# Charges of an attention block: repeated over partitions through memory in place of copies and transposes, with new ranks for the order of work

## The chip, the cores and the metric

The kernel runs on one core of a Trainium2 chip, in one launch. Its time is the device time in microseconds; shown are medians of several runs. Its engines are TensorE (PE; the loading of its weights is shown apart as PEld), VectorE (DVE), ScalarE (ACT), GpSimd (POOL) and SyncE (SP), which here does nothing but issue DMAs. Each engine runs its own list of instructions in a fixed order and waits where an operand is not ready.

## The reference

Two blocks with residuals, in float32, over x of 32 x 512 x 256:

```python
# attention; b, n, d = 32, 512, 256
q     = tanh(x @ W_charge.T + b_charge)[..., 0]        # one charge per token
phi_c = mags * q[..., None] ** arange(5)               # its powers 0..4
shell = normalize(x @ W_shell.T + b_shell)             # 64 per token
proj  = shell @ omega.T + rff_bias                     # 32 per token
phi_s = concat([cos(proj), sin(proj)]) * rff_scale     # 64 per token
tp    = (phi_c[..., :, None] * phi_s[..., None, :]).reshape(b, n, 320)
phi   = tp @ W_combine.T                               # 64 per token
logits = einsum('bnd,bmd->bnm', phi, phi) * T / temp   # T: decay by distance
attn  = softmax(where(causal, logits, -inf))
out   = (attn @ (x @ W_v.T + b_v)) @ W_out.T + b_out
# slots
h     = gelu(concat([x, mean of S]) @ w1.T + b1)
alpha = softmax over the top 8 of 64 of (h @ w2.T + b2), else 0
slot_input = einsum('bts,btd->bsd', alpha, x) / sums   # 64 slots per batch
S_new = GRU(slot_input, S)
out   = (alpha @ (S_new @ wv.T + bv)) @ wo.T + bo
# the whole
x = x + attention(layernorm(x));  x = x + slots(layernorm(x))
```

The charge q of a token multiplies 64 values of the same token. Where the 64 values lie along the partitions, q has to be there 64 times too.

## The kernel before

The 32 batches are worked in 16 groups of two (`GB = 2`). A group has 2 x 512 tokens, `GT = 8` tiles of 128 tokens. W_out is folded into W_v in the setup, wv and wo likewise.

*Tokens and angles of a group g.* Loads bring x (and, from group 2 on, a second copy xb that VectorE transposes to xT, L876; in the first two groups TensorE does it, pta L853). TensorE projects each token tile: pf, 128 x 321 = 64 shell values, one charge before tanh, 256 values of V (L906). VectorE scales by the layernorm's statistics (bna, L786) and adds the bias: sv (L919), with tokens on the partitions. Then two strands run from sv:

- *The charges.* POOL copies the charge column 64 times, for two half-batches next to each other (qrep, L945, four copies of 128x128); TensorE transposes these in four pieces (ptq, L965), which puts 64 equal rows per half on the partitions; ACT makes Tanh (L975) and Square (L983) of the 128x512 result: qs.
- *The angles.* POOL squares the shell (sq, L992), VectorE sums (rn, L1006), POOL takes the power -1/2 (L1012, L1013), VectorE scales (shn, L1020, two halves), TensorE transposes (pts, L1036) and multiplies by omega (pp, L1053, tiles of 64x64), ACT adds the bias (ang, L1066), VectorE brings into one turn (L1077, L1078), ACT takes the Sin (L1085).

The two meet on VectorE in the powers (L1099, two instructions): tp = phases x q, x q². TensorE combines five powers (pph, L1111, 40 matmuls of 64x64 tiles), VectorE multiplies by part of the decay (phi, L1126).

*Attention.* Four row blocks per batch: logits pl (L1165), masked with their extremes by VectorE (lg, L1194), Exp on ACT (pr, L1206), transposed by TensorE (ptp, L1243) and copied by ACT (prT, L1261), times V (po, L1249), added to x by VectorE (L1278).

*Slots.* Second layernorm (lnb on POOL, xm on ACT, L1301), transposed (ptb L822, xmT L834), ph (L1328), gelu h_t (L1339), router logits prr (L1353) with their transposes rlT and prt (L1359, L1367, L1376), the top 8 by VectorE (top, L1384), their softmax on ACT and VectorE (L1393 to L1411) and al on POOL (L1418). Then psi (slot_input, L1442), gi and its transpose pt_gi (L1466), the GRU's gates prz and pn (L1492), hn (L1553) with its transpose pt_hn, al transposed (pta, L1563), pv (L1580), py (L1600), the add to x (L1614) and the store (L1619).

*The order of the work.* Nothing runs in the order in which the code is written. `Plan.add` (L126) collects steps, each with an engine, a cost, the steps it comes after and the buffers it uses. `Plan.order` (L150 to L240) gives each a rank,

```python
at = (1.0 - LATE) * s.at + LATE * (longest - s.tail)
s.rank = s.g * STRIDE + at + delay + late * max(0, s.g - last + 3)
```

where `s.at` is the earliest start within the group by the costs (with HOP for each change of engine), `s.tail` the work behind it, and delay and late come from `DELAY` for each of twelve stages. Then it simulates: of the steps whose inputs are there it places the one that could start first, among equals the one of lowest rank (TABLE is what another ACT table costs in this simulation, SWITCH what is added to a PE step's rank that has another tile shape). Buffers come from pools of fixed sizes (`SLOTS_OF`, L53). The list that results is emitted as it stands (L1645 to L1647). So a group's work overlaps with that of its neighbours, and with other costs or ranks all engines' lists come out otherwise, also far from the line that was changed.

Nearly all DMAs are on SP's list: the setup's weights (L277), x and xb, and the stores. A few weights are on ACT's and POOL's.

Of the kernel before, what the change touches and what calls it, by code (L numbers as in the profile page):

```python
# [11 lines left out]
AF = mybir.ActivationFunctionType  # L12
# [3 lines left out]
P = 128  # L16
D = 256
KD = D // P
T = 512
HT = T // 2  # L20
NT = T // P
GB = 2
GT = GB * NT
# [4 lines left out]
PHI_S = 2 * RFF  # L28
# [19 lines left out]
C_Q = SHELL  # L48
# [16 lines left out]
    "prT": 3,  # L65
    "h_t": 2,
    "qs": 1,
    "row": 7,
    "half": 4,
}  # L70


HOP = 0.41
TABLE = 1.28
SWITCH = 1.77
STRIDE = 26.98
LATE = 0.0

DELAY = {
    "setup": (0.0, 0.0),  # L80
    "load": (4.9, -6.0),
    "tokens": (10.7, 1.0),
    "angles": (-1.4, -34.3),
    "phi": (3.9, 0.9),
    "weights": (-3.0, 1.9),
    "values": (17.8, -4.4),
    "normal": (17.2, 16.3),
    "router": (34.1, 12.7),
    "taken": (-19.4, 7.1),
    "gru": (-29.8, 4.8),  # L90
    "given": (20.5, 17.4),
}

SPARE = 3
# [149 lines left out]
def block_kernel(ctx: ExitStack, tc: tile.TileContext, a: dict, out: bass.AP):  # L244
    nc = tc.nc
# [10 lines left out]
    def lazy(tag, name, shape, dtype=F32):  # L256

        if tag not in pools:
            kind = {"space": bass.MemoryType.PSUM} if tag == "ps" else {}
# [77 lines left out]
    ident = const("ident", [P, P])  # L337
# [52 lines left out]
    s_ident = add("POOL", 0.5, make_ident, rank=-41.0)  # L390
# [138 lines left out]
    for q in range(P // SQ):  # L529
        for k in range(KD):  # L530
# [9 lines left out]
                    land=4.0,  # L540
# [348 lines left out]
    def features(g):  # L889
# [45 lines left out]

        qrep = lazy("row", f"qrep_{g}", [P, GB, NT // 2, 2, PHI_S])
        sq = lazy("row", f"sq_{g}", [P, GT, SHELL])
        rn = small(f"rn_{g}", [P, GT])  # L940
        shn = lazy("row", f"shn_{g}", [P, NT, GB, SHELL])
        def repeated(bb):
            for h in range(2):
                lo = bb * NT + (h ^ bb) * (NT // 2)
                nc.gpsimd.tensor_copy(  # L945
                    qrep()[:, bb, :, h, :],
                    sv()[:, lo : lo + NT // 2, C_Q : C_Q + 1].to_broadcast([P, NT // 2, PHI_S]),
                )

        s_rep = [  # L950
            add(
                "POOL",
                0.63,
                lambda bb=bb: repeated(bb),
                s_sv[bb * NT : (bb + 1) * NT],
                [qrep, sv],
            )
            for bb in range(GB)
        ]
        ptq = bank(f"ptq_{g}")  # L960
        qs = lazy("qs", f"qs_{g}", [P, 2, T])

        def charges_turned():
            for c in range(NT):
                nc.tensor.transpose(  # L965
                    ptq()[:, c * P : (c + 1) * P],
                    qrep()[:, c // 2, c % 2].rearrange("p h s -> p (h s)"),
                    ident,
                )

        s = add("PE", 0.45, charges_turned, s_rep + [s_ident], [qrep, ptq, qs])
        s = add(
            "ACT",
            0.61,
            lambda: nc.scalar.activation(qs()[:, 0, :], ptq(), AF.Tanh),  # L975
            [s],
            [ptq, qs],
            "exp",
        )
        s_q = add(  # L980
            "ACT",
            0.62,
            lambda: nc.scalar.activation(qs()[:, 1, :], qs()[:, 0, :], AF.Square),  # L983
            [s],
            [qs],
        )

        s_sq = [
            add(
# [21 lines left out]
        def norms():  # L1011
# [80 lines left out]
        for m in (1, 3):  # L1092

            def powers(m=m):
                if m == 1:
                    a, b = tp()[:, 0:1, :].to_broadcast([P, 2, T]), qs()
                else:
                    a, b = tp()[:, 1:3, :], qs()[:, 1:2, :].to_broadcast([P, 2, T])
                nc.vector.tensor_tensor(tp()[:, m : m + 2, :], a, b, ALU.mult)  # L1099
# [6 lines left out]
        def combined():  # L1106
            for m in range(ORDER + 1):
# [32 lines left out]
    def attention(g, sv, s_sv, phi, s_phi):  # L1140
# [8 lines left out]
        for tiles in ((0, 1), (2,), (3,)):  # L1149
# [34 lines left out]
            for bb in range(GB):  # L1184
                lg = lazy("lg", f"lg_{n}_{bb}", [P, T])
                pr = lazy("pr", f"pr_{n}_{bb}", [P, T])
                prs.append(pr)
                for i in tiles:
                    nm = small(f"nm_{g}_{bb}_{i}", [P, 1], bufs=8)
                    w = (i + 1) * P  # L1190
                    c = slice(off[i], off[i] + w)

                    def lowest(bb=bb, w=w, c=c, pls=pls, lg=lg, nm=nm):
                        nc.vector.tensor_tensor_reduce(  # L1194
                            out=lg()[:, c],
                            in0=pls[bb]()[:, c],
                            in1=mask[:, T - w : T],
                            scale=1.0,
                            scalar=TOP,
                            op0=ALU.add,  # L1200
                            op1=ALU.min,
                            accum_out=nm(),
                        )
# [226 lines left out]
    def slots(g, xm, al, s_al):  # L1430
# [161 lines left out]
        for c2 in range(NT // 2):  # L1592
# [16 lines left out]
            for bb in range(GB):  # L1609
# [97 lines left out]
```

## Time and profile before

| | |
|---|---|
| time, median of 3 runs | 717.17 us (716.65 to 717.93) |
| time of the profiled execution | 716.61 us |
| its span | 714.8 us |
| granted clock of TensorE, mean | 0.993 |
| busy: PE | 686.8 us (96%) |
| busy: DVE / ACT / POOL | 595.3 / 422.5 / 236.2 us |
| ptq (L965), 64 transposes of 128x128 | 9.7 us by durations, 274 ns each (they overlap) |
| qrep (L945), 64 copies on POOL | 17.8 us, 294 ns each |
| Tanh L975 / Square L983, 16 each on ACT | 9.7 / 10.2 us |
| powers (L1099), 32 on DVE | 39.4 us, 1231 ns each |
| DMA moved | 53.76 MB |

A group's row in the profile gives: line, engine, operation, output <- inputs, shapes, count, then busy time in all, the mean of one in ns, and after the bar how long the engine stood idle just ahead of these instructions and for whom. Idle time matters only on the engine that sets the end at that place. Rows of matmuls (PE) give durations from start to end; as matmuls overlap, the pitch from one to the next is shorter. In a chain row, "PE pl L1165 x16" is a run of 16 instructions of one kind, with its start and its length.

### The profile page before, as it was taken

Reading aid. Unit: us, or ns where it says so; the run is one execution under the profiler, and the core shown is the slowest. Engines: PE = TensorE matmul, PEld = TensorE weight load, DVE = VectorE, ACT = ScalarE, POOL = GpSimd, SP = SyncE. Lnnn points to the kernel's source line nnn. Section 1 sums busy time; section 2 is a strip of 40 time slices with the busy share of each in tenths; the row PEclk is TensorE's granted clock in tenths of the full one; section 3 lists DMA queues with packets and bytes.
Section 4 is the critical chain, followed back from the end, with each engine's and each line's share of the span. In section 5 each row is a group of like instructions: output and inputs, shape, how many; then the busy total and the mean of one; then the engine's idle time right before and its main releaser. Section 6 shows DMA issues by size and latency. Waiting matters only on the chain.

```text
span 714.8 us, 12300 instructions
## 1 busy us (share of the span) xinstructions
PE 686.8 (96%) x4170; PEld 480.2 (67%) x4170; DVE 595.3 (83%) x1750; ACT 422.5 (59%) x867; POOL 236.2 (33%) x470
## 2 busy tenths in 40 slices
PE   3989999999999999999999999999999999999884
PEld 3757676767676766767676776767667676777453
DVE  3999888789798989979897979979899887878474
ACT  1445849585755747656565856467475655758720
POOL 3640532214334432324324133423423243321120
PEclk9999999999999999999999999999999999999989
DMA  6796113032304223331412333131330301001013
GB/s 179 161 278 121 34 26 60 2 118 58 119 2 115 63 60 118 60 120 25 94 59 60 119 60 118 27 93 60 59 118 1 118 1 60 1 1 60 0 60 118
DMA packets 100016, 53.76 MB, mean 75 GB/s; under 512 B 64017, under 2 KB 99153, under 8 KB 99953
## 3 DMA queue, kind: packets, MB, share of 16 engines
q1 hardware_dynamic: 98640, 52.45, 28.3%
q8 instruction: 33, 0.54, 0.3%
q10 hardware_dynamic: 1104, 0.36, 0.2%
q0 software_dynamic: 208, 0.17, 0.2%
q14 instruction: 31, 0.25, 0.1%
HBM read 35.85 MB, written 16.78 MB: 74 GB/s over the span
## 4 chain that ended last, share of the span: by engine, by line
PE 89%; DVE 4%; ACT 2%; DMA 2%; issue 1%; POOL 1%; DVEq 0%; ACTq 0%; POOLq 0%
PE po L1249 20%; PE pf L906 18%; PE ph L1328 7%; PE pl L1165 5%; PE pph L1111 5%; PE ptp L1243 5%; PE psi L1442 4%; PE py L1600 4%; PE ptb L822 4%; PE prz L1492 4%; PE pv L1580 2%; PE prr L1353 2%; PE pn L1492 2%; PE pta L1563 1%; DMA x<-in_x_dram 1%; PE pp L1053 1%
## 5 line engine op out<-in xcount | busy, mean ns | idle before, releaser
L1249 PE MATMUL po<-sv,prT 128*128 128x256 f32 x640 | 149.6, 380 | 0.0
L906 PE MATMUL pf<-wfb,xT 128*128 128x321 f32 x448 | 133.2, 439 | 0.0
L1249 PEld LDWEIGHTS po<-sv,prT 128*128 128x128 f32 x640 | 117.0, 189 | 22.6 <-issue 5.9
L906 PEld LDWEIGHTS pf<-wfb,xT 128*128 128x128 f32 x448 | 80.4, 190 | 37.5 <-issue 6.8
L1301 ACT ACTIVATE xm<-x,lnb 128x256 f32<-128x256 f32 x128 | 66.0, 594 | 43.3 <-POOL lnb L807 43.3
L1206 ACT ACTIVATE pr<-lg,nm 128x128 f32<-128x128 f32 (+3 forms) x128 | 70.7, 555 | 13.1 <-DVE nm L1194 9.8
L1278 DVE SCALAR_TENSOR_TENSOR x<-po,den,x 128x256 f32<-128x256 f32 x128 | 60.3, 475 | 20.3 <-PE po L1249 20.0
L945 POOL COPY qrep<-sv 128x128 f32<-128x128 f32 x64 | 17.8, 294 | 154.1 <-DVE sv L919 154.1
L919 DVE SCALAR_TENSOR_TENSOR sv<-pf,lna,bias_f 128x321 f32<-128x321 f32 x128 | 63.8, 543 | 4.3 <-PE pf L906 3.9
L1194 DVE CUSTOM_DVE_ANT_0 lg<-pl,mask 128x128 f32<-128x128 f32 (+3 forms) x128 | 55.9, 487 | 6.9 <-PE pl L1165 6.8
L1328 PE MATMUL ph<-xmT,w1x 128*128 128x512 f32 x128 | 59.5, 596 | 0.0
L786 DVE BATCH_NORM_STATS2 bnb<-x 128x6 f32<-128x256 f32 x128 | 53.3, 424 | 3.1
L1261 ACT COPY prT<-ptp 128x384 f32<-128x384 f32 (+1 forms) x96 | 45.9, 517 | 4.9 <-PE ptp L1243 4.7
L786 DVE BATCH_NORM_STATS2 bna<-x 128x6 f32<-128x256 f32 x128 | 46.9, 413 | 0.0
L1243 PE MATMUL ptp<-ident,pr 128*128 128x128 f32 x320 | 45.4, 274 | 0.4 <-ACT pr L1206 0.3
L1243 PEld LDWEIGHTS ptp<-ident,pr 128*128 128x128 f32 x320 | 37.1, 140 | 8.5 <-ACT pr L1206 2.4
L1614 DVE TENSOR_TENSOR x<-py,x 128x512 f32<-128x512 f32 x64 | 39.9, 684 | 3.3 <-PE py L1600 3.0
L834 ACT COPY xmT<-ptb 128x512 f32<-128x512 f32 x64 | 33.3, 589 | 15.8 <-PE ptb L822 15.8
L1165 PE MATMUL pl<-phi 64*128 64x256 f32 (+1 forms) x384 | 42.4, 356 | 0.0
L797 POOL TENSOR_TENSOR lnb<-bnb 128x8 f32<-128x8 f32 x16 | 9.8, 612 | 94.4 <-DVE bnb L786 94.4
L1099 DVE TENSOR_TENSOR tp<-tp,qs 128x1024 f32<-128x1024 f32 x32 | 39.4, 1231 | 1.3 <-ACT tp L1085 0.7
L876 DVE STREAM_TRANSPOSE xT<-xb 128x512 f32<-128x512 f32 x56 | 38.2, 695 | 0.5 <-issue 0.4
(171 smaller groups left out, 1291.7 us busy)
## 6 DMA issues: line engine op xcount, KB each, us to landing
x<-in_x_dram SPq DMA_DIRECT2D x32, 512.0 KB, 4.8
out_dram<-x SPq DMA_DIRECT2D x64, 256.0 KB, 2.5
xb<-in_x_dram SPq DMA_DIRECT2D x112, 128.0 KB, 3.4
setup<-in_gru_whh_t_dram SPq DMA_DIRECT2D x1, 768.0 KB, 4.6
wih<-in_gru_wih_t_dram SPq DMA_DIRECT2D x1, 768.0 KB, 7.9
wfb<-wf SPq DMA_DIRECT2D x8, 40.1 KB, 3.4
setup<-in_W_v_dram SPq DMA_DIRECT2D x1, 256.0 KB, 3.5
setup<-in_W_out_t_dram ACTq DMA_DIRECT2D x1, 256.0 KB, 9.2
```

The costliest lines, as they stand in the source:

```text
L786: lambda t=t: nc.vector.bn_stats(st()[:, t, :], src()[:, t, :]),
L906: nc.tensor.matmul(pf()[:, 0:NF], tile_()[:, k, c * P : (c + 1) * P], w[:, k, :], start=(k == 0), stop=(k == KD - 1),)
L919: lambda t=t, pf=pf: nc.vector.scalar_tensor_tensor(sv()[:, t, :], pf()[:, 0:NF], ln()[:, 1, t : t + 1], bias_f, ALU.mult, ALU.add,),
L1165: nc.tensor.matmul(pls[bb]()[:, off[i] + lo : off[i] + lo + w], phi()[r, 0, q : q + P], phi()[r, 1, k : k + w], start=True, stop=True,)
L1194: nc.vector.tensor_tensor_reduce(out=lg()[:, c], in0=pls[bb]()[:, c], in1=mask[:, T - w : T], scale=1.0, scalar=TOP, op0=ALU.add, op1=ALU.min,
L1206: nc.scalar.activation(pr()[:, c], lg()[:, c], AF.Exp, bias=nm(), scale=-1.0, accum_out=den()[:, tiles.index(i), bb : bb + 1],)
L1243: nc.tensor.transpose(pt()[:, j : j + P], prs[bb]()[:, j : j + P], ident)
L1249: nc.tensor.matmul(po()[:, d * D : (d + 1) * D], pr_t()[:, lo : lo + P], sv()[:, bb * NT + j, C_V:NF], start=(j == 0), stop=(j == i),)
L1261: lambda width=width, pt=pt, pr_t=pr_t: nc.scalar.copy(pr_t()[:, 0:width], pt()[:, 0:width]),
L1278: nc.vector.scalar_tensor_tensor(xt()[:, t, :], po()[:, d * D : (d + 1) * D], den()[:, d, bb : bb + 1], xt()[:, t, :], ALU.mult, ALU.add,)
L1301: lambda t=t: nc.scalar.activation(xm()[:, t, 0:D], xt()[:, t, :], AF.Identity, bias=ln()[:, 4, t : t + 1], scale=ln()[:, 1, t : t + 1],),
L1328: nc.tensor.matmul(ph(), w1x[:, k, :], tiles[k](), start=(k == 0), stop=(k == KD - 1))
```

## The change

The charges and their squares are made on the narrow form, tokens on the partitions, 8 columns per group: ACT's Tanh reads sv's charge column (128x8), a Square follows, into qc. SP stores qc to a small tile in the chip's memory, qd, in token order: 2 x 2 x 512 values of 4 bytes, where neighbours in memory come from neighbouring partitions. Four reads on SP bring it back into qs, each to 64 partitions from the same 2 x 256 values (64 x 2 KB = 128 KB). The powers wait for all four. The four POOL copies, the four transposes with their PSUM bank and the two wide activations of each group are gone. There are two qd tiles and, as before, one qs.

The planner's constants are others too: HOP, SWITCH, STRIDE, LATE and all of DELAY, and the costs of four kinds of VectorE steps. They alter the order on all engines.

```diff
@@ SLOTS_OF
     "qs": 1,
+    "qd": 2,
...
-HOP = 0.41
+HOP = 0.65
 TABLE = 1.28
-SWITCH = 1.77
-STRIDE = 26.98
-LATE = 0.0
+SWITCH = 1.57
+STRIDE = 23.49
+LATE = 0.83
...
 DELAY = {
     "setup": (0.0, 0.0),
-    "load": (4.9, -6.0),
-    "tokens": (10.7, 1.0),
-    "angles": (-1.4, -34.3),
-    "phi": (3.9, 0.9),
-    "weights": (-3.0, 1.9),
-    "values": (17.8, -4.4),
-    "normal": (17.2, 16.3),
-    "router": (34.1, 12.7),
-    "taken": (-19.4, 7.1),
-    "gru": (-29.8, 4.8),
-    "given": (20.5, 17.4),
+    "load": (5.6, -11.7),
+    "tokens": (-1.8, -13.0),
+    "angles": (-0.8, -5.4),
+    "phi": (17.1, 3.6),
+    "weights": (29.9, -16.3),
+    "values": (27.9, -17.7),
+    "normal": (-0.4, -1.6),
+    "router": (36.0, 14.4),
+    "taken": (-24.9, -2.4),
+    "gru": (25.5, -10.5),
+    "given": (27.0, -5.8),
 }
...
-        qrep = lazy("row", f"qrep_{g}", [P, GB, NT // 2, 2, PHI_S])
...
-        def repeated(bb):
-            for h in range(2):
-                lo = bb * NT + (h ^ bb) * (NT // 2)
-                nc.gpsimd.tensor_copy(
-                    qrep()[:, bb, :, h, :],
-                    sv()[:, lo : lo + NT // 2, C_Q : C_Q + 1].to_broadcast([P, NT // 2, PHI_S]),
-                )
...
-        s = add("PE", 0.45, charges_turned, s_rep + [s_ident], [qrep, ptq, qs])
+        qc = small(f"qc_{g}", [P, 2, GT])
+        qd = lazy("qd", f"qd_{g}", [2, GB, T])
+        qs = lazy("qs", f"qs_{g}", [P, 2, GB, HT])
         s = add(
             "ACT",
-            0.61,
-            lambda: nc.scalar.activation(qs()[:, 0, :], ptq(), AF.Tanh),
+            0.25,
+            lambda: nc.scalar.activation(qc()[:, 0, :], sv()[:, :, C_Q], AF.Tanh),
+            s_sv,
+            [sv, qc],
+            "exp",
+        )
+        s = add(
+            "ACT",
+            0.2,
+            lambda: nc.scalar.activation(qc()[:, 1, :], qc()[:, 0, :], AF.Square),
             [s],
-            [ptq, qs],
-            "exp",
-        )
...
+        s = add(
+            "SP",
+            0.6,
+            lambda: nc.sync.dma_start(
+                out=qd().rearrange("m b (c p) -> p (m b c)", p=P),
+                in_=qc().rearrange("p m t -> p (m t)"),
+            ),
             [s],
-            [qs],
-        )
+            [qc, qd],
+            land=3.5,
+        )
+        s_q = []
+        for h in range(2):
+            for bb in range(GB):
+
+                def repeated(h=h, bb=bb):
+                    lo = (h ^ bb) * HT
+                    nc.sync.dma_start(
+                        out=qs()[h * PHI_S : (h + 1) * PHI_S, :, bb, :],
+                        in_=qd()[:, bb, lo : lo + HT].partition_broadcast(PHI_S),
+                    )
+
+                s_q.append(add("SP", 0.6, repeated, [s], [qd, qs], land=3.0))
...
-                0.4,
+                0.35,
                 lambda bb=bb: nc.vector.tensor_tensor(
                     shn()[:, :, bb, :],
...
-            s_tp.append(add("DVE", 1.25, powers, [s_tp[-1], s_q], [tp, qs]))
+            s_tp.append(add("DVE", 1.25, powers, [s_tp[-1]] + s_q, [tp, qs]))
...
-                0.42,
+                0.35,
                 lambda h=h, n=n, dec=dec: nc.vector.tensor_tensor(
                     phi()[:, n, h * HT : (h + 1) * HT],
...
-                        "DVE", 0.17 + 0.12 * (i + 1), lowest, [s_pl, s_mask], [pls[bb], lg, nm]
+                        "DVE", 0.11 + 0.12 * (i + 1), lowest, [s_pl, s_mask], [pls[bb], lg, nm]
...
-                s_y = add("DVE", 0.65, added, [s], [pys[bb], xt])
+                s_y = add("DVE", 0.6, added, [s], [pys[bb], xt])
```

More of the change, by code (lines that the diff above doesn't have):

```diff
@@ L258, in lazy @@
         if tag not in pools:
-            kind = {"space": bass.MemoryType.PSUM} if tag == "ps" else {}
+            space = {"ps": bass.MemoryType.PSUM, "qd": bass.MemoryType.DRAM}.get(tag)
+            kind = {"space": space} if space else {}
             pools[tag] = ctx.enter_context(
@@ L941, in features @@
         shn = lazy("row", f"shn_{g}", [P, NT, GB, SHELL])
-        def repeated(bb):
-            for h in range(2):
-                lo = bb * NT + (h ^ bb) * (NT // 2)
-                nc.gpsimd.tensor_copy(
-                    qrep()[:, bb, :, h, :],
-                    sv()[:, lo : lo + NT // 2, C_Q : C_Q + 1].to_broadcast([P, NT // 2, PHI_S]),
-                )
[L950 to L956, printed above, removed]
-            )
-            for bb in range(GB)
-        ]
@@ L960, in features @@
[L960 to L968, printed above, removed]
-                )
-        s = add("PE", 0.45, charges_turned, s_rep + [s_ident], [qrep, ptq, qs])
+        qc = small(f"qc_{g}", [P, 2, GT])
+        qd = lazy("qd", f"qd_{g}", [2, GB, T])
@@ L972, in features @@
+        qs = lazy("qs", f"qs_{g}", [P, 2, GB, HT])
         s = add(
             "ACT",
-            0.61,
-            lambda: nc.scalar.activation(qs()[:, 0, :], ptq(), AF.Tanh),
-            [s],
-            [ptq, qs],
+            0.25,
+            lambda: nc.scalar.activation(qc()[:, 0, :], sv()[:, :, C_Q], AF.Tanh),
+            s_sv,
+            [sv, qc],
             "exp",
         )
-        s_q = add(
+        s = add(
             "ACT",
-            0.62,
-            lambda: nc.scalar.activation(qs()[:, 1, :], qs()[:, 0, :], AF.Square),
+            0.2,
+            lambda: nc.scalar.activation(qc()[:, 1, :], qc()[:, 0, :], AF.Square),
@@ L984, in features @@
             [s],
-            [qs],
+            [qc],
         )
+        s = add(
[5 more added lines that the diff above has]
+            ),
+            [s],
+            [qc, qd],
[11 more added lines that the diff above has]
+                s_q.append(add("SP", 0.6, repeated, [s], [qd, qs], land=3.0))
@@ L1094, in powers @@
             def powers(m=m):
+                q = qs().rearrange("p m b t -> p m (b t)")
                 if m == 1:
-                    a, b = tp()[:, 0:1, :].to_broadcast([P, 2, T]), qs()
+                    a, b = tp()[:, 0:1, :].to_broadcast([P, 2, T]), q
                 else:
-                    a, b = tp()[:, 1:3, :], qs()[:, 1:2, :].to_broadcast([P, 2, T])
+                    a, b = tp()[:, 1:3, :], q[:, 1:2, :].to_broadcast([P, 2, T])
                 nc.vector.tensor_tensor(tp()[:, m : m + 2, :], a, b, ALU.mult)
-            s_tp.append(add("DVE", 1.25, powers, [s_tp[-1], s_q], [tp, qs]))
+            s_tp.append(add("DVE", 1.25, powers, [s_tp[-1]] + s_q, [tp, qs]))
         plan.stage = "phi"
```

## The prediction

> **What bounds the kernel now.** I read the page's first part, then the busy time by stretches, then the chain of work that ended last. The page's first part, busy time by engine:
>
> ```profile
> PE 686.8 (96%) x4170; PEld 480.2 (67%) x4170; DVE 595.3 (83%) x1750; ACT 422.5 (59%) x867; POOL 236.2 (33%) x470
> ```
>
> Two stretches (length; busy time and count of PE, PEld, DVE, ACT, POOL; granted clock, DMA share, GB/s):
>
> ```profile
> 60.00:655.00 595.00, 594.96 (x3696) 420.88 (x3695) 514.89 (x1516) 376.54 (x778) 199.94 (x392) 1.00 0.25 64
> 655.00:714.80 59.80, 45.26 (x224) 26.56 (x222) 33.27 (x107) 23.26 (x43) 10.91 (x19) 0.94 0.15 53
> ```
>
> From 60 to 655 us TensorE is busy 594.96 of 595 us at full clock: there the time is the sum of its matmuls' pitches, and what other engines save is worth nothing. The rest is the fill (first matmul at 11.1 us, PE not dense before 60) and the drain (14.5 us of PE idle after 655).
>
> The chain inside the dense stretch (start, length, what):
>
> ```profile
> 275.37 2.36 PE pf L906 x8
> 277.73 1.72 PE pl L1165 x16
> ...
> 285.44 0.59 PE pta L1563 x4
> 286.02 0.33 PE ptp L1243 x3
> 286.35 0.44 PE ptq L965 x4
> 286.79 0.22 PE pt_gi L1466 x2
> ...
> 318.06 2.17 PE pf L906 x8
> ```
>
> All are PE pieces, each starting where the last ends. The transposes that go, ptq, are one piece of 0.44 us in each of 16 groups. The two pf pieces hold eight equal matmuls; the one of 2.17 us follows ptb, of the same 128x128 tile shape, the one of 2.36 us follows pl, with tiles of 64 rows. So a change of tile shape in PE's order costs 0.19 us. Over all 168 changes from 60 to 655 us the matmuls' starts in the trace stand 30.7 us over their plain pitches: **0.183 us each**.
>
> **The change, part by part.** The sum is made against the profiled span of 714.8 us. That run took 716.6, 1.8 us of it outside the span; the median shown is 717.17. So time = span + 2.4.
>
> *Removed.* From the groups by line:
>
> ```profile
> L983 ACT ACTIVATE qs<-qs 128x512 f32<-128x512 f32 x16 | 10.2, 639 | 0.3
> ...
> L965 PE MATMUL ptq<-ident,qrep 128*128 128x128 f32 x64 | 9.7, 274 | 0.0
> L975 ACT ACTIVATE qs<-ptq 128x512 f32<-128x512 f32 x16 | 9.7, 605 | 1.2 <-PE ptq L965 1.1
> ```
>
> PE: 16 x 0.44 = **-7.1 us**, on the path (the 274 ns overlap; the chain's 0.44 for four counts). POOL's 64 copies of 294 ns (17.8 us) and ACT's 32 wide activations (19.9 us) lie beside a dense PE, as does the PSUM bank that comes free: 0.
>
> *Added, narrow Tanh and Square (128x8).* No row is that narrow; nearest are the setup's 128x1 activations, 0.20 to 0.24 us: 32 x 0.21 = 6.7 us of ACT. Six more table loads (60 in the program's order for 54; 1.283 us each) add 7.7. ACT ends 5.5 us lighter at 59% busy: 0. Behind the Tanh stand two xmT copies, the router's Exp and the softmax; it waits for sv of the last token tile, done 0.5 us after the pf end, before ACT has made the xmT copies ahead of it (+3.0): it holds nobody up.
>
> *Added, the write (16 x 8 KB) and reads (64 x 128 KB) on SP.* From the page's DMA parts:
>
> ```profile
> q10 hardware_dynamic: 1104, 0.36, 0.2%
> ...
> out_dram<-x SPq DMA_DIRECT2D x64, 256.0 KB, 2.5
> xb<-in_x_dram SPq DMA_DIRECT2D x112, 128.0 KB, 3.4
> ```
>
> The reads have xb's size: 3.4 us to landing, after four issues of 0.5. The write moves 2048 single elements of 4 bytes, 128 on each of 16 engines; before writes no elements to memory. Nearest is ACT's queue, where 384 of 1104 packets have 4 bytes: 0.2% of 16 x 714.8 us over 1104 = 21 ns a packet. 128 x 21 ns = 2.7, on a store's 2.5: **5.2 us**. The Trainium skill speaks against this write: "DMA: Bandwidth & Descriptors", Rules for kernel authors, turns a strided last dimension into one descriptor per element, and by its Specifications an engine reads, modifies and writes below 512 B. If that doubles the packet's time, landing is an estimated 8 us; from below 2.5. I take 5.2, by the nearer row.
>
> Is it hidden? In the new PE order of a middle group, counted from the end of the eight pf, PE does pt_hn 0.22, pl 1.0, ptb 1.75, pl 0.8, two ph 3.44, pv 0.86, ptp 0.87, pl 0.8, pts 0.44, psi 1.89, py and pp 2.5, pt_gi and pta 0.7, ptp 0.33, po 1.73, prz 1.72 = 19.0 us. Then VectorE does rz (0.65) and reaches the powers, the first user of qs: 19.7. The write goes out at 3.0 + two narrow activations 0.4 + issue 0.5 = 4, lands at 9.2 (12 by the rule), reads + 2.0 + 3.4: **14.6 us, or 17.4 by the rule, against 19.7**. Both make the sum 0. The cover is 10.3 us of write landing; past it VectorE stands, with the statistics of x behind it. On SP xb loads and stores stand behind the write and reads; they are of a group not yet due: 0.
>
> *Moved: new ranks, tile shapes.* In the two programs' PE orders I count 192 changes of tile shape before and 227 after (a steady group has 15 for 12.5: pl in three pieces, py in two). 35 x 0.183 = **+6.4 us**.
>
> *The steady order otherwise.* Two PE steps stand close to their makers. psi (10.3 us after the pf) needs the router's weights: VectorE's work from the pf's end to the sums is 7.5 us, with pitches 0.08 under the rows' durations, and POOL's al 1.04: 8.6. pts (at 9.8) needs shn, done at 8.2. Slack 1.6 us each. I take **+1.0 us** of stalls for the run, range 0 to 13 (1 us in 13 groups).
>
> *The fill.* In the timeline of before:
>
> ```profile
> 38.04 0.89 SPq L277 DMA_DIRECT2D bv<-in_bv_dram  x1
> ...
> 43.20 2.47 DVE L1099 TENSOR_TENSOR tp<-tp,qs 128x1024 f32<-128x1024 f32 x2
> ```
>
> SP now waits at the first write for ACT (to 30.6 us: xT of group 1 and a table load come first) and at the second for sv of group 1 and its Square (39.5). bih_n, bhh, wih, wv, wo and bv stand behind: bv goes out some 5.5 us later and lands near 49 for 45.9, and in the new VectorE order its user stands ahead of phi of group 0. rn of group 1 stands ahead of the powers, which end at 46.9 for 45.6. The second reads (behind three xb, issued to 51) land near 55; VectorE waits for them with logits of group 0 behind it, PE at pph of group 1. That ends at 58 to 59.5, with 11.2 us of ptp and po of group 0 still to do and one stall of 1.8; in before it ends at 70.0 with those done. **+2.3 us**, from 0 (landings 2 us quicker) to +5 (write at 8 us).
>
> *The drain.* After its last po before needs 58 us, in turn through PE, ACT, VectorE and POOL. The new order has pv and py of group 12 (2.8 us) behind that po and one more ptb (0.44) ahead of it: these fall into PE's waits. psi of group 15 comes 36 us after the last po in both. **-2.5 us**, from -2.8 to 0.
>
> Sum: 714.8 - 7.1 + 6.4 + 1.0 + 2.3 - 2.5 = 714.9 us of span; + 2.4 = **717.3 us**: no change. A difference of under 0.2% (1.4 us) a measurement of this kernel can't tell from none.
>
> **The rivals.**
> - *The ends are better than I make them.* The fill costs nothing, no stalls, the drain gives 2.8: 714.8 - 7.1 + 6.4 - 2.8 = 711.3, time 713.7. For it: PE's idle time lies at the ends, and the new ranks move just these orders. Against: two new waits on SP ahead of the setup's weights.
> - *VectorE comes late in each group.* The 1.6 us at psi and pts are used up and PE stalls 0.25 to 1 us in 13 groups: 719.5 to 729. For it: 514.89 of 595 us busy, and three xT transposes now stand before the sums. Against: before had the same load without a stall.
> - *The write lands late: slower.* Place: the powers of groups 2 to 14. VectorE meets it from a landing of 10.3 us on, and has 13% of a group's 41.5 us, 5.4, to catch up. From 15.8 us each further us costs 13 us: at 17, + 16, time 733. For it: 2048 single elements, of which no row exists. Against: it needs 104 ns a packet, five times the row's.
> - *PE's work isn't taken away.* Excluded: the program has 64 transposes fewer.
>
> **How the numbers follow.** Forecast 0.48, own range 713.5 to 719.5 (of it 0.20 faster, 0.22 same, 0.06 slower); better ends 0.12; late VectorE 0.26; late write 0.14. Faster 0.32, same 0.22, slower 0.46. The 8-in-10 range leaves out the late write, the last 0.03 of the late VectorE and 0.03 below: 712.5 to 728.
>
> **What would show it.** No ptq; pf in one piece of eight; PE dense from about 62 us, with a two-group period of 83.1 as before (-0.9 of ptq, +0.9 of changes); 227 changes of tile shape; the write landing in 4 to 8 us; VectorE waiting for the reads in groups 0 and 1 alone; SP waiting for ACT at the first two writes; 58 us from the last po to the end. The forecast is wrong if VectorE waits for the reads or PE for shn or al in every group, if the changes of shape cost PE much less than 0.18 us, or if PE's density begins after 66 us.

## The result: 765.62 us, and where 48 us of it lie

The changed kernel takes 765.62 us (763.87 to 768.14, four runs) for 716.91 before: a ratio of 1.0679, 95% interval 1.0645 to 1.0714. Forecast was 717.3, range 712.5 to 728. The forecast is wrong. The suspect of its rival "The write lands late" is the right one, but the loss is not where that rival put it, as will be seen.

The profiled execution has a span of 762.8 us for 714.8, + 48.0. First the busy time by engine:

```profile
PE 701.0 (92%) x4106; PEld 483.9 (63%) x4106; DVE 599.6 (79%) x1750; ACT 417.0 (55%) x873; POOL 208.0 (27%) x406
```

TensorE has 64 matmuls fewer, as said, and is busy longer: part of its work ran at a lower clock (mean granted clock 0.975, for 0.993 before). Then the stretches (length; busy time and count of PE, PEld, DVE, ACT, POOL; granted clock, DMA share, GB/s):

```profile
0.00:60.00 60.00, 36.69 (x190) 25.52 (x190) 35.11 (x91) 14.40 (x28) 22.39 (x51) 0.90 0.55 127
60.00:92.00 32.00, 23.26 (x153) 18.27 (x154) 24.49 (x69) 11.22 (x29) 2.84 (x7) 0.81 0.87 206
92.00:655.00 563.00, 547.50 (x3215) 378.09 (x3217) 463.10 (x1335) 331.85 (x690) 162.11 (x313) 0.99 0.31 75
```

PE is dense only from about 92 us, for 60 before, and even then idles 15.5 us of 563. A good mark for both is the first pf matmul of a group. Group 2's stands at 69.9 us before and at 91.8 after (+21.9); from there to group 13's it is 442.9 us before and 468.3 after (+25.4, or 2.3 per group); from there to the end 201.9 and 202.7 (+0.8). So about half of the loss is in the fill and half in the steady stretch. What new waits there are, in the waits view (engine, line, waited for: us in total, times, longest):

```profile
DVE bna L788 <- DMA x<-in_x_dram: 32.7, 14, 6.6
...
DVE tp L1099 <- DMA qs<-qd: 4.9, 6, 1.3
```

The powers (tp), where that rival put the loss, wait 4.9 us in the whole run. VectorE waits 32.7 us at bna, for the loads of **x**, which the change doesn't touch; before, it never waited there. And in the DMA part of the page (KB each, median us from issue to landing):

```profile
out_dram<-x SPq DMA_DIRECT2D x64, 256.0 KB, 3.3
xb<-in_x_dram SPq DMA_DIRECT2D x112, 128.0 KB, 6.3
qs<-qd SPq DMA_DIRECT2D x64, 128.0 KB, 3.4
...
qd<-qc SPq DMA_DIRECT2D x16, 8.0 KB, 11.8
```

A transfer of 8 KB takes 11.8 us to land. The reads behind it take 3.4 as forecast; but xb's loads take 6.3 for 3.4 before. These medians rest on few records: the profile has the landing of 2 of the 16 writes and of 12 of xb's 112 loads. SP's own list bears the 11.8 out. The reads wait for the write, and in 15 of the 16 groups the first of them goes out 11.2 to 12.9 us after the write (18.8 in the second group).

How the one leads to the other is seen in SP's list in a steady group:

```profile
266.61 0.37 SPq L966 DMA_DIRECT2D qd<-qc  x1
269.95 1.92 SPq L279 DMA_DIRECT2D xb<-in_x_dram  x4
278.83 2.53 SPq L980 DMA_DIRECT2D qs<-qd  x4
281.46 2.13 SPq L279 DMA_DIRECT2D xb<-in_x_dram  x4
283.71 2.39 SPq L1619 DMA_DIRECT2D out_dram<-x  x4
289.66 0.93 SPq L279 DMA_DIRECT2D x<-in_x_dram  x2
```

and in the chain of work that ended last (start, length, what):

```profile
285.34 0.19 DVE rz L1505
285.54 3.97 DMA out_dram<-x
...
290.09 4.80 DMA x<-in_x_dram
...
294.92 1.41 DVE bna L788 x4
```

SP stands from 272 to 278.8 us until the write has landed. Behind the reads come four loads of xb and the four stores of an older group, and behind these the load of the next x, which needs the buffer (one of five) that the stores set free: store 4.0 us, load 4.8 us, and at the moment of landing VectorE, already waiting, starts that group's statistics.

### The profile page after: what moved, and what is told of

The parts are those of the page before. It is cut to its first block, busy times and chain, and to the rows that moved or that the text cites. A ratio compares the mean times of both kernels' runs of the same rounds, so it can differ in the third digit from the quotient of the medians.

```text
span 762.8 us, 12245 instructions
## 1 busy us (share of the span) xinstructions
PE 701.0 (92%) x4106; PEld 483.9 (63%) x4106; DVE 599.6 (79%) x1750; ACT 417.0 (55%) x873; POOL 208.0 (27%) x406
## 4 chain that ended last, share of the span: by engine, by line
PE 35%; DVE 29%; DMA 23%; ACT 4%; issue 4%; SPq 4%; POOL 1%; DVEq 0%; ACTq 0%
PE po L1249 8%; DMA x<-in_x_dram 7%; DMA qd<-qc 6%; DVE sv L921 4%; DMA out_dram<-x 4%; PE psi L1442 3%; PE py L1600 3%; DVE rest L1385 3%; PE ph L1328 3%; PE pf L908 3%; DVE x L1278 3%; PE pl L1165 2%; PE prz L1492 2%; DVE bnb L788 2%; DVE bna L788 2%
## 5 line engine op out<-in xcount | busy, mean ns | idle before, releaser
L908 PE MATMUL pf<-wfb,xT 128*128 128x321 f32 x448 | 126.5, 440 | 2.3 <-ACT rl L1376 2.1
L908 PEld LDWEIGHTS pf<-wfb,xT 128*128 128x128 f32 x448 | 84.6, 191 | 41.3 <-issue 2.7
L1206 ACT ACTIVATE pr<-lg,nm 128x512 f32<-128x512 f32 (+3 forms) x128 | 70.9, 557 | 10.8 <-DVE nm L1194 10.7
L788 DVE BATCH_NORM_STATS2 bna<-x 128x6 f32<-128x256 f32 x128 | 45.6, 413 | 32.8 <-DMA x<-in_x_dram 32.7
L1278 DVE SCALAR_TENSOR_TENSOR x<-po,den,x 128x256 f32<-128x256 f32 x128 | 60.1, 473 | 13.2 <-PE po L1249 13.2
L921 DVE SCALAR_TENSOR_TENSOR sv<-pf,lna,bias_f 128x321 f32<-128x321 f32 x128 | 67.2, 542 | 1.1 <-PE pf L908 0.9
L1538 POOL TENSOR_TENSOR nn<-nn,rh 128x256 f32<-128x256 f32 x16 | 11.6, 727 | 192.5 <-DVE rh L1529 179.9
L1194 DVE CUSTOM_DVE_ANT_0 lg<-pl,mask 128x256 f32<-128x256 f32 (+3 forms) x128 | 56.2, 479 | 5.0 <-PE pl L1165 5.0
L1165 PE MATMUL pl<-phi 64*128 64x256 f32 (+1 forms) x384 | 52.3, 369 | 5.1 <-ACT xmT L836 4.8
L1614 DVE TENSOR_TENSOR x<-py,x 128x512 f32<-128x512 f32 x64 | 40.4, 683 | 11.4 <-PE py L1600 11.4
L1165 PEld LDWEIGHTS pl<-phi 64*128 64x128 f32 x384 | 33.4, 188 | 20.1 <-ACT xmT L836 7.4
L799 POOL TENSOR_TENSOR lna<-bna 128x8 f32<-128x8 f32 x16 | 5.2, 324 | 124.5 <-DVE bna L788 124.5
L824 PE MATMUL ptb<-ident,xm 128*128 128x128 f32 x256 | 37.8, 289 | 1.1 <-ACT xm L1301 0.8
```

The costliest lines, as they stand in the source:

```text
L788: lambda t=t: nc.vector.bn_stats(st()[:, t, :], src()[:, t, :]),
L908: nc.tensor.matmul(pf()[:, 0:NF], tile_()[:, k, c * P : (c + 1) * P], w[:, k, :], start=(k == 0), stop=(k == KD - 1),)
L921: lambda t=t, pf=pf: nc.vector.scalar_tensor_tensor(sv()[:, t, :], pf()[:, 0:NF], ln()[:, 1, t : t + 1], bias_f, ALU.mult, ALU.add,),
L1165: nc.tensor.matmul(pls[bb]()[:, off[i] + lo : off[i] + lo + w], phi()[r, 0, q : q + P], phi()[r, 1, k : k + w], start=True, stop=True,)
L1194: nc.vector.tensor_tensor_reduce(out=lg()[:, c], in0=pls[bb]()[:, c], in1=mask[:, T - w : T], scale=1.0, scalar=TOP, op0=ALU.add, op1=ALU.min,
L1206: nc.scalar.activation(pr()[:, c], lg()[:, c], AF.Exp, bias=nm(), scale=-1.0, accum_out=den()[:, tiles.index(i), bb : bb + 1],)
```

## The experiments

Each ratio is to the kernel before, run again beside the experiment (medians of 716.67 to 717.37 us).

Theories at the outset: **W**, the element-wise write's landing is the cause; **R**, the new ranks alone are (statistics right behind the load of x, with five buffers' turnover setting the period); **B**, it takes both.

### One part alone

```diff
 # the kernel before, with these lines of the change only
+HOP = 0.65; SWITCH = 1.57; STRIDE = 23.49; LATE = 0.83; DELAY = {...}
+# and the four planner costs of VectorE steps
```

> The kernel before with the changed kernel's planner constants and step costs; its copies, transposes and wide activations are as before. Theory W (the element-wise write, 11.8 us to landing, keeps SP, and with it stores and loads of x, waiting): without the write the ranks cost little, 714 to 722 us. Theory R (the new ranks put a group's statistics right behind the load of its x, and that load behind the store that frees its buffer, so a group's stay in the five x buffers sets the period): 740 to 765 us. Theory B (both are needed: a long landing in an order without slack): 714 to 725 us here, and no loss in the other half (old ranks) either.

Measured: 741.48 us, ratio 1.0336 (1.0309 to 1.0362).

```diff
 # the changed kernel, with before's planner constants and costs
-HOP = 0.65; SWITCH = 1.57; STRIDE = 23.49; LATE = 0.83; DELAY = {...}
+HOP = 0.41; SWITCH = 1.77; STRIDE = 26.98; LATE = 0.0; DELAY = {...}
```

> The changed kernel's write and reads, with the planner constants and step costs of before. W: slow as the change, 740 to 790 us. R: 64 transposes fewer and no new order, 708 to 720 us. B: 708 to 725 us.

Measured: 761.41 us, ratio 1.0623 (1.06 to 1.0646). The new path is slow in the old order as well, so R can't be the whole. But W's 714 to 722 for the old path was missed by 20 us too, and 741.48 lies in R's range. R's mechanism isn't there, though: VectorE waits 0.5 us in all for x. The loss is spread over the run (4.5 us by the start of group 2, 13.2 from there to group 13, 4.9 behind it). With the new path in the old order VectorE waits 22.8 us at the powers, for the reads, and 2.7 for x: there the late write harms the user that the rival in the forecast named. The ranks and the path are not independent, and neither of the two runs isolates its half. So from here on the engines' lists were held fixed where that could be done.

### The write made cheap, and doubled, in the same order

```diff
-                out=qd().rearrange("m b (c p) -> p (m b c)", p=P),
+                out=qd().rearrange("m b t -> (m b t)").rearrange("(p k) -> p k", p=P),
```

> The changed kernel with every engine's list as it is, only the write lays each partition's 16 values side by side (128 pieces of 64 bytes in place of 2048 of 4; the values then come back in another order, so the output is not the reference's; all work is done). Landing 2 to 3 us for 11.8. W: the loss goes, 714 to 725 us. R: 755 to 766 us. B: 714 to 730 us.

Measured: 722.16 us, ratio 1.0068 (1.0051 to 1.0084). In its page's DMA part:

```profile
out_dram<-x SPq DMA_DIRECT2D x64, 256.0 KB, 2.4
xb<-in_x_dram SPq DMA_DIRECT2D x112, 128.0 KB, 3.5
...
qd<-qc SPq DMA_DIRECT2D x16, 8.0 KB, 1.5
```

The same bytes in pieces of 64 land in 1.5 us, and **43.5 of the 48.7 us are gone**. VectorE no longer waits for x. SP's list in a steady group of this run:

```profile
281.96 0.34 SPq L966 DMA_DIRECT2D qd<-qc  x1
283.91 2.80 SPq L279 DMA_DIRECT2D xb<-in_x_dram  x4
286.75 2.53 SPq L980 DMA_DIRECT2D qs<-qd  x4
289.38 2.13 SPq L279 DMA_DIRECT2D xb<-in_x_dram  x4
293.40 2.63 SPq L1619 DMA_DIRECT2D out_dram<-x  x4
298.05 0.93 SPq L279 DMA_DIRECT2D x<-in_x_dram  x2
```

The reads follow the write by 4.8 us for 12.2. Here x is issued 16 us after the write, for 23 above, and VectorE takes up its bna at 305.6: the first half of x has landed at 301.5 (3.5 us after its issue), so that is 4.1 us after the landing. In the steady groups of this run it is 3.5 to 4.1 us. That is all the slack the new order has; the order before has 4.2 to 9.2.

```diff
+            for d in (qx, qd):     # qx: a second tile, read by nobody
                 nc.sync.dma_start(
                     out=d().rearrange("m b (c p) -> p (m b c)", p=P),
```

> The changed kernel with the same element-wise write made once more, into a second tile that nobody reads, ahead of the one that is read; orders otherwise the same. The landing should become some 21 us. W: about as much again as the change lost, 795 to 830 us. R: 765 to 775 us. B: 790 to 830 us.

Measured: 880.6 us, ratio 1.2281 (1.2255 to 1.2307); the second write lands 20.0 us after its issue (one landing is on record; in SP's list the reads follow the first write by 18.2 to 21.9 us in 15 of 16 groups). That is 50 us above W's range, for now the powers do wait:

```profile
DVE tp L1105 <- DMA qs<-qd: 90.0, 13, 10.7
DVE bna L788 <- DMA x<-in_x_dram: 44.3, 13, 12.7
```

which is the mechanism of the forecast's rival, set going by twice its write. So W holds for the change, and R as a sole cause has fallen. So has B as it was put: it had no loss in the old order, where the new path lost 44 us.

### Is it the wait on SP, or the DMA engines?

The landing can do harm in two ways: SP stands until it is there (**Q**), or the 2048 small writes hold up the DMA engines that other transfers need (**J**).

```diff
 # write in rows as above; behind each group's fourth read:
+                        nc.sync.dma_start(
+                            out=qx().rearrange("m b (c p) -> p (m b c)", p=P),
+                            in_=qc().rearrange("p m t -> p (m t)"),
+                        )
```

> The kernel with the write in rows (722.2 us; the values come back in another order, so the output is not the reference's), and behind each group's four reads the element-wise write of 2048 values once more, into a tile that nobody reads: the DMA engines are filled as in the changed kernel, but no read stands waiting for that write on SP. Theory Q (the loss is SP standing before the reads until the write has landed, with stores and loads behind): 722 to 730 us. Theory J (the loss is the DMA engines, held up by the small writes, so that loads of x and xb and stores land late): 750 to 770 us.

Measured: 783.24 us, ratio 1.0911 (1.0857 to 1.0965). Worse than the change itself and above J's range, though SP waits for no slow write:

```profile
out_dram<-x SPq DMA_DIRECT2D x64, 256.0 KB, 7.2
```

The stores, which here come right behind the small writes, land in 7.2 us for 2.4 (24 of 64 on record), and VectorE waits 50.7 us for x.

```diff
 # write in rows as above, reached through four more small transfers
+            c, a, b = qc().rearrange("p m t -> p (m t)"), qq()[:, 0:16], qq()[:, 16:32]
+            for o, i in ((rows(qx), c), (a, rows(qx)), (rows(qy), a), (b, rows(qy)), (rows(qd), b)):
+                nc.sync.dma_start(out=o, in_=i)
```

> The kernel with the write in rows, but the values go to memory and back twice before the tile that is read is written: five small transfers of 128 pieces of 64 bytes, each waiting for the one before (the output is not the reference's). The reads are let go some 9 to 12 us after the first of them goes out, as in the changed kernel, but the DMA engines carry almost nothing more. Q: 750 to 770 us. J: 722 to 733 us.

Measured: 741.32 us, ratio 1.033 (1.0312 to 1.0349). Between Q's range and J's. The reads go out 9.7 us after the first transfer (in the change: 12.4; means of the writes 5 to 12):

```profile
297.25 0.34 SPq L972 DMA_DIRECT2D qx<-qc  x1
...
306.67 2.53 SPq L981 DMA_DIRECT2D qs<-qd  x4
...
317.28 0.93 SPq L279 DMA_DIRECT2D x<-in_x_dram  x2
```

Group 2's pf stands at 88.4 us for 74.7 with the plain rows (+13.7; the change: +17.1), but from there on a group costs what it does in rows (447.8 us to group 13, for 446.2). So **SP's wait alone costs most of the fill's loss**; the setup's weights stand behind it. In the steady stretch this wait was still within the slack, just (VectorE waits 9.9 us for x over 12 groups, none over 3.6).

The change waits 2.7 us longer, and that is past the slack. From the first transfer of the write to the load of x, SP's list has 15.8 us with plain rows, 20.0 here and 22.8 in the change (the same means); with 16 us and a slack of 4, the edge is at 20. Behind the reads nothing is longer in the change: x goes out 10.8 us after them, here 10.6 (medians), and no wait in the change is for xb. So in the change's steady stretch Q is enough, and a part of J in it isn't shown. The jam run shows what such writes do to stores right behind them; in the change the stores come when the write has landed. A wait of 12 us without small writes was not run, so this stands on the times of these lists.

```diff
-            lambda: nc.sync.dma_start(          # the write
+            lambda: nc.scalar.dma_start(
```

> The changed kernel with the write issued by ScalarE, on its own queue, in place of SP's; the reads stay on SP and wait for it there. If the small writes hold up the DMA engines for every queue: 755 to 772 us, xb loads landing in 5 us or more. If they hold up their own queue alone: 735 to 750 us (SP's wait remains, worth 19 us in the run that had it alone), xb landing in 3.5 us.

Measured: 784.97 us, ratio 1.097 (1.0895 to 1.1044); slower than either expectation, and slower than the change. That run's profile has no landing times, but its DMA packets show it. Packets of 256 bytes (xb's) that began in each us, in a steady group; the write went out on ScalarE's queue at 268.4 us, xb's loads on SP's at 270.9:

```
write_from_act   us 272: 0   273: 33   274: 19   275: 152   276: 119   277: 114   278: 88   279: 107   280: 164   281: 867
write_in_rows    us 284.5: 449   285.5: 538   286.5: 548   287.5: 513
```

The write's packets, 2064 with 4 bytes each, had all ended by 270.6 us (each is shown with 7 to 9 ns), and until 281 the loads on the **other** queue crawl at about a fifth of their pace. So such a write holds up the loads of another queue too, and its packets' times in the trace do not contain it. Whether the place is the engines or the memory, no run tells. This run is 19 us slower than the change with the same elements: here x goes out 23.7 us after the write, for 22.8. Why that is so, and why it costs this much, wasn't settled.

### How much of a landing is too much

```diff
-                out=qd().rearrange("m b (c p) -> p (m b c)", p=P),
-                in_=qc().rearrange("p m t -> p (m t)"),
+                out=qd().rearrange("m b (c p k) -> p (m b c) k", p=P, k=2),
+                in_=qc().rearrange("p m (t k) -> p (m t) k", k=2),
```

> The changed kernel with pairs of values side by side in memory: 1024 pieces of 8 bytes for 2048 of 4 (the values come back in another order, so the output is not the reference's). Landing, from 11.8 us for 2048 and 20.0 for 4096 pieces: 7.5 us if the price is one per piece, 11 to 12 if it is one per byte. Time on a straight line between 722 (landing 1.5) and 765.6: 747 us; if there is a threshold below which all is hidden: 722 to 730 us.

Measured: 728.36 us, ratio 1.0157 (1.0128 to 1.0186), and

```profile
qd<-qc SPq DMA_DIRECT2D x16, 8.0 KB, 5.6
```

The bytes are the same as in the change and the landing is less than half, so the price goes by the piece, not by the byte. And there is a threshold. From group 2 to 13 it is 446.2 us, exactly as in rows: a landing of 5.6 costs the steady stretch nothing (x goes out 17.0 us after the write, and 1.3 to 3.8 us of slack are left), one of 11.8 costs it 22. Only the fill is later, by 6.6 us.

```diff
+                out=(rows form) if g < 2 else qd().rearrange("m b (c p) -> p (m b c)", p=P),
```

> The changed kernel with the write in rows in groups 0 and 1 alone (there the output is not the reference's), element-wise from group 2 on. If the loss is in two parts, that of the fill goes: matmuls of group 2 started at 91.8 us in the change, at 74.7 with all writes in rows, so 748 us (744 to 752). If the fill's delay is made up later anyway: 762 to 767 us. If all comes from the fill: 722 to 728 us.

Measured: 756.1 us, ratio 1.0551 (1.0521 to 1.0581). Missed: group 2's pf is back at 73.8 us, 18.0 earlier than in the change, but only 9.5 us of that reach the end. From group 2 to 13 it is now 475.4 us, for 468.3 in the change: the steady loss grew by 7. SP's list shows where: the reads follow the write by 13.1 us for 12.4 in the change, and x goes out 23.7 us after it for 22.8. Why the write takes longer there isn't shown. So the two parts exist, but they don't add.

### A finer write in a plan of its own

```diff
+            lambda: nc.vector.transpose(qq()[:, SQ : 2 * SQ], qq()[:, 0:SQ]),   # 32x32 squares
...
+            for k in range(P // SQ):
+                nc.sync.dma_start(
+                    out=qd().rearrange("m b (c k i) -> k (m b c) i", c=NT, i=SQ)[k],
+                    in_=qq()[k * SQ : k * SQ + 2 * GT, SQ : 2 * SQ],
+                )
```

> The changed kernel, but VectorE transposes the 16 narrow columns in 32x32 squares ahead of the write, so that 128 bytes lie side by side in memory (four writes of 16 pieces, the same data; planner constants of the change). The extra step moves the order: 205 changes of tile shape for 227. Theory W: landing some 2 us, no loss by the write, 714 to 722 us. Were it not the element size of the write: 755 to 770 us.

Measured: 757.97 us, ratio 1.0562 (1.0536 to 1.0588).

> The same with the planner constants and step costs of before (188 changes of tile shape for before's 192). 64 transposes fewer are worth 7.1 us, four changes 0.7; the fill may take 0 to 4 and SP's sixteen times four more issues nothing. W: 708 to 716 us. If it is the ranks or the path itself that cost the time: 740 us or more.

Measured: 731.96 us, ratio 1.0206 (1.0184 to 1.0228).

Both missed, and by the ranges set beforehand 757.97 speaks against W: it lies where the time was to lie if the element size were not the cause. But the four writes land in 1.6 and 1.4 us and VectorE never waits for x, so the waits of the change are not what costs the time here. The added VectorE step led the planner to other orders. With the new ranks PE then waits 2 to 4 us in several groups between the router's transposes and the ptp behind them (3.6 us at 306.6, 2.6 at 522.5); with the old ranks the steady stretch is the shortest so far (438.7 us from group 2 to 13, for 442.9 before), but from group 13 to the end it is 17.7 us longer, with 10.5 us in one place in which PE waits for POOL's al ahead of a late psi. That the new order is the whole cause of the two misses isn't shown. The evidence for W is the runs with fixed lists.

### The path alone, in before's order

```diff
         def charges_turned():
+            if narrow:                       # g >= 2
+                c = sv()[:, :, C_Q].unsqueeze(1).to_broadcast([P, 2, GT])
+                nc.scalar.activation(col(0), c, AF.Tanh)
+                nc.scalar.activation(col(1), col(0), AF.Square)
+                return
...
+        def first():                         # in the place of the wide Tanh: VectorE's
+            ...                              # transpose and the four writes, as above
+        def second():                        # in the place of the wide Square: the four reads
```

> The kernel before with its own planner constants, its plan laid out with the old steps and costs; from group 2 on the copies and transposes issue nothing, and in their places in the order stand the narrow Tanh and Square, VectorE's transpose in squares, four writes of 16 pieces of 128 bytes and the four reads (groups 0 and 1 as before). So the order of the rest stays, 192 changes of tile shape as before, and the term of the prediction for the work taken from TensorE stands alone: 14 x 0.44 = 6.1 us less, 711 us (709 to 713). Were the saving given back elsewhere (the reads late for the powers, SP's issues): 716 us or more.

Measured: **711.02 us**, ratio 0.9916 (0.9889 to 0.9943), under 1% faster than the kernel before, and faster than the change by 55 us. Its stretches:

```profile
0.00:70.00 70.00, 56.05 (x322) 40.47 (x326) 56.05 (x149) 26.34 (x53) 25.34 (x59) 0.98 0.81 188
70.00:655.00 585.00, 584.79 (x3602) 410.81 (x3596) 510.13 (x1521) 364.56 (x777) 186.29 (x341) 1.00 0.29 77
```

PE is dense from 70 us on. From group 2 to 13 it takes 438.3 us for 442.9 before, 0.42 per group, with the ptq transposes gone (0.436 us per group) and the pitch sums of every other tile in PE's steady stretch within 0.001 us per group of before (groups 7 to 13). VectorE's transpose takes 199 ns, writes land in 1.4 us, reads in 3.1, and the powers don't wait. The idea of the change holds; its gain is what the forecast's first term said.

## Why the prediction was wrong, step by step

The three stretches of the runs side by side (from the starts of the first pf matmuls of groups 2 and 13; us):

| kernel | write lands in | x goes out after the write (mean of writes 5 to 12) | start of group 2 | to group 13 | to the end | VectorE waits for x | time |
|---|---|---|---|---|---|---|---|
| before | - | - | 69.9 | 442.9 | 201.9 | 0 | 716.9 |
| write in rows | 1.5 | 15.8 | 74.7 | 446.2 | 199.5 | 0 | 722.2 |
| pieces of 8 | 5.6 | 17.0 | 81.3 | 446.2 | 200.4 | 0 | 728.4 |
| wait alone | 1.4 (reads let go after 9.7) | 20.0 | 88.4 | 447.8 | 200.4 | 9.9 | 741.3 |
| **changed kernel** | 11.8 | 22.8 | 91.8 | 468.3 | 202.7 | 32.7 | 765.6 |
| jam alone | 1.4, the second 12.0 | 24.9 | 94.5 | 483.1 | 204.9 | 50.7 | 783.2 |

- *Removed, -7.1:* right. In before's order 14 of 16 groups gave 5.7 us of the 6.1 expected.
- *The write, "landing 5.2 us", 8 by the rule:* **the first step that failed**, in size. It is 11.8. The row taken as nearest was of another kind of transfer, loads on ACT's queue, and its 21 ns is the mean of all that queue's packets; those of 4 bytes are shown with 9 ns. Nor is the price in a packet's record at all: the change's write is in the trace as 2064 packets of 4 bytes, one for each of the 2048 elements and 16 more, of 7 to 9 ns, over in 1.3 us. By the landings (1.5 us for 128 pieces, 11.8 for 2048) each of the 128 pieces on an engine costs an estimated 80 ns, if they are spread evenly over 16 engines; 64 ns by the 1024 pieces of 8 bytes. The rule, weighed and set aside, pointed the right way; doubled, it was still short. Why a piece costs so much no run shows.
- *"On SP xb loads and stores stand behind the write and reads; they are of a group not yet due: 0":* **the step that failed in kind**, and the costlier one in the steady stretch. I had measured the cover at the first user of the data, the powers: 10.3 us, direct cost from 15.8. There it held: at 11.8 they wait 4.9 us in all, at 20.0 they wait 90. But behind the reads stand the stores, behind the stores the load of the x that takes their buffer, and the new order puts that x's statistics some 4 us behind its landing. I listed "stores" among what is queued and didn't ask what a store lets go. The cover there ends between the 9.7 us of wait alone, at which a group loses next to nothing, and the change's 12.4.
- *Not in the sum at all:* that the small writes hold up other transfers. xb's loads land later in the change, but no engine is seen waiting for them, so in the steady stretch this term can't be told from nothing. By these times the step before it carries what the 25.4 us from group 2 to 13 are over the 3.3 of the order alone (the rows). In the fill it may be part of the 3.4 us that the change loses more than wait alone.
- *The fill, +2.3 (0 to 5):* the mechanism right (SP stands at the first two writes, the setup's weights behind), the size not: 21.9. Of that 4.8 come with rows; 17.1 are the landing's. SP was held at the first reads to 42.7 us for 35.4 in rows, then by the second write and queue, so that wo's weights went out at 51.8 instead of 42.4, and took 15.6 us to land. In SP's list and the waits of the change, then of the rows:

```profile
42.72 2.57 SPq L980 DMA_DIRECT2D qs<-qd  x4
51.83 7.12 SPq L279 DMA_DIRECT2D setup<-in_wo_t_dram  x1
PE pw L444 <- DMA setup<-in_wo_t_dram: 11.7, 1, 11.7
```

```profile
35.44 2.57 SPq L980 DMA_DIRECT2D qs<-qd  x4
42.39 0.47 SPq L279 DMA_DIRECT2D setup<-in_wo_t_dram  x1
PE pw L444 <- DMA setup<-in_wo_t_dram: 2.6, 1, 2.6
```

  Even at about the landing I had assumed (5.2; the pieces of 8 take 5.6) the fill is 11.4 us late, so this term would have been wrong by 9 with the right write.
- *Changes of tile shape, +6.4:* count right (227), sum low. In rows, whose steady period is even (41.9 us for 41.55), the sums of PE pitches per group against before, in us:

| | ptq | pl | py | pts | ptp | ptb | others | sum |
|---|---|---|---|---|---|---|---|---|
| per group | -0.44 | +0.50 | +0.20 | +0.15 | +0.11 | +0.10 | -0.31 | +0.31 |

  Without ptq the order costs 0.75 us per group more, not the 0.46 that 2.5 changes at 0.183 give. pl, in three pieces for one or two, is most of it; how much of that is the price of a change of shape and how much the shorter pieces themselves isn't separated. So "no change" in the period was wrong too: +0.3 per group.
- *Stalls, +1.0:* right for the order as such (in rows PE idles 1.5 us from 92 to 655 us). In the change PE waits at pl (4.8 us from 92 to 655 us), pts (4.8) and ptb (0.8), behind VectorE and ACT, which are late. A stretch of it (idle time before the instruction and who ended it, in brackets), and below it the stretches from 266 us:

```profile
265.80 0.92 PE L1165 MATMUL pl<-phi 64*128 64x256 f32 x6 [1.04 <-ACT xmT L836]
266.64 1.92 PE L824 MATMUL ptb<-ident,xm 128*128 128x128 f32 x8
268.35 2.78 PE L1328 MATMUL ph<-xmT,w1x 128*128 128x512 f32 x4
```

```profile
266.00:268.00 2.00, 2.00 (x13) 1.83 (x12) 2.00 (x5) 1.07 (x5) 0.87 (x1) 0.69 0.16 1
268.00:270.00 2.00, 2.00 (x5) 1.03 (x4) 2.00 (x7) 1.73 (x4) 1.01 (x2) 0.50 0.30 3
```

  After this wait of 1.0 us the granted clock falls to 0.50 for 3.4 us, and the ph matmuls stand 0.85 us apart for 0.43: the wait costs nearly three. Not each one does. From 92 to 655 us the change has five waits of 1.04 or 1.05 us, and two of them were followed by such a fall; a third fall came with a wait of 2.1 us at 208.8. The three falls cost an estimated 5 us (half of three times 3.4).
- *The drain:* 58 us from the last po to the end, as said (58.3). The 2.5 us of gain in it can't be told apart in these runs.
- *The rivals:* "the write lands late" gave 733 at a landing of 17 and thought 104 ns a packet too much; the right suspect with the wrong victim. "VectorE comes late" had the right engine, and named psi and pts; VectorE was late, but for x (from 92 to 655 us PE then did wait 4.8 us at pts, but only 0.6 at psi).

What stays open: why the two ranks and paths crossed lose 24 and 44 us in detail, what of the change's loss the held-up transfers have beside SP's wait, why the write from ScalarE's queue is dearer than from SP's, and why a write takes longer where the fill is earlier.

## What to carry to other kernels

Price a transfer by its pieces, not by its bytes: here 8 KB in 2048 pieces took 11.8 us to land, half a megabyte of x 4.7, and loads on another queue slowed down with it. A time per packet is no price for a landing. When a wait enters a queue, follow each instruction behind it to what it releases (store, buffer, load, statistics) and measure the slack there, not only at the first user of the new data. And where a planner orders the program, test the idea in the old order first: that run gave the sum's first term to within half a microsecond, while each re-planned version mixed the idea with another order.

## What the runs showed of the hardware that was not expected

- The packets of an element-wise write to memory were over at once (the change: all within 1.3 us, 7 to 9 ns each), and the write landed late: 5.6 us for 1024 pieces of 8 bytes, 11.8 for 2048 of 4, while 128 pieces of 64 bytes took 1.5. The DMA share doesn't contain that time: from 269 to 279 us in the change, with the write still under way, it is 0.10.
- Until such a write had landed, loads on another queue ran at about a fifth of their pace (write from ScalarE's queue: some 110 packets of 256 bytes per us from 275 to 281 us, for 512 in the run with rows).
- Two of the five TensorE waits of 1.04 or 1.05 us in the change's steady stretch were followed by 3.4 us at half the granted clock.
